# A mixture-of-experts and conditioning layer on one core: products on zeros ahead of the first input, later loads behind the decoded weights, routing and sorting in two groups of blocks

## The chip, the core and the metric

The kernel runs on one core of a Trainium2 chip. A core has five engines that run their own instruction streams beside each other: TensorE (matrix products, PE in the profile; PEld are its weight loads), VectorE (DVE), ScalarE (ACT), GpSimd (POOL) and SyncE (SP), which here only issues DMA transfers. The metric is the device time of one launch in microseconds; the median over several runs is given. A profile is one execution of its own, with a time of its own.

## The reference, cut to what matters

`x` has 128 sequences of 32 tokens with 128 features, 4096 tokens in all. Two layers are added to it.

```python
def _L0_cond_ref(x, mu, W_dec, b_dec, V):          # a weight matrix for each sequence
    U = (mu @ W_dec + b_dec).reshape(B, 129, 30)
    param = einsum('bik,kj->bij', U, V)
    return einsum('bsd,bde->bse', x, param[:, :-1, :]) + param[:, -1, :][:, None, :]

def _L0_ffn_ref(x, Wg, bg, W1, b1, W2, b2):        # 8 experts, the best 2 for each token
    topk_scores, topk_idx = top_k(xf @ Wg.T + bg, 2)
    w = softmax(topk_scores, axis=-1)
    h = gelu(einsum('td,ehd->teh', xf, W1) + b1)
    o = einsum('teh,eoh->teo', h, W2) + b2
    return einsum('tko,tk->to', take_along_axis(o, topk_idx[:, :, None], axis=1), w)

x = x + _L0_ffn_ref(_L0_cond_ref(x, cond_512, ...), ...)
x = x + _L1_ffn_ref(_L1_cond_ref(x, ids, ...), ...)
```

`_L1_cond_ref` is a chain of layernorms, table lookups by token ids and a two-layer network; `_L1_ffn_ref` is a gated network 128 to 512 to 512 to 512 to 128.

## The kernel before, in words

**Blocks.** The tokens are handled in 8 blocks of 512 (`TB`). For the first 3 blocks (`ND`) all 8 experts are computed densely ("dense experts", `experts`, L1143). For the other 5 (`NS`) the tokens are sorted by expert: each token's row of 64 values is scattered to `z_rows` in DRAM at the place of its expert, the experts run over their own rows (`sorted_expert`, L1189; it loads `zr`, makes `pzr`, `phs`, `py`, stores `y_rows`), and the results are gathered back (`combined`, L1252, `yg`). Then every block goes through `conditioning` (L1280) and `feed_forward` (L1418).

**The front.** It runs in these steps:

- Loads (L553 to L580): `mu_t` and `pre` on ScalarE's queue, all others on SP's, in this order: `w_dec` in two pieces, `x_t` in two pieces, `moe_w1`, `vecs`, `tabs`, `moe_w2`, `int_w1`, `st_in`, `wide_w2`, `b2_rows`, `tab_b`, a store of zeros to `z_rows`, and `tab_pw`. GpSimd clears the tile `zeros` (L575) first of all.
- Decoding (L617 to L639): four chunks of products `pu` of `w_dec` and `mu_t`, each with two PSUM tiles that VectorE and ScalarE copy to `u_sb`.
- `conditioned(i)` (L690) for each block: products `pz` of the block's `x_t` with `pre` and `u_sb` (outputs of 32 rows), VectorE's sum `zq`, products `pq` (which hold the block's 30 values a token and its 8 gate values), and for the first 3 blocks the transposes `p4_i` (shown as `p` in the profile) that give `z4`.
- `folded_all` (L665): four products `pwv` of `moe_w1`, 512 columns each, which ScalarE and VectorE turn into `w4`.
- Routing (L789) for blocks 0 to 2 and then once for blocks 3 to 7: VectorE adds the gate bias, finds the best two experts (`m_a`, `at_a`, `lo_a`, `hot_a`, then the same with `_b`), and `token_weights` (L826) makes their weights, with one `Exp` on ScalarE.
- `sorted_z` (L769) copies the values of blocks 3 to 7 out of `pq` to `z_tok`; `sorting` (L864) counts, for all 20 groups of 128 tokens at once, how many tokens go to each expert (`both`, two products `p_rank` and `p_count`, five doubling sums `sums`), and makes each token's row (`row_z` for the scatter, `row` for the gather).
- `scatters` (L954): 40 indirect DMAs on GpSimd, one for each 128 tokens and each of their two experts. A small memset `tick` behind each orders them.

**What sets the order.** All operations are recorded in a plan. `Plan.ordered` (L361) puts them in an order with a simple model of costs (`cost`, L307): at each step it takes, over all engines, the operation that can start first, and among those of one engine that can start within 20 ns the one with the lowest `prio`. The result is one fixed instruction stream for each engine. `prio` comes from where the code stands; in the front it is set by `in_order` (L90), which spreads the steps of a stream over a stretch, and after the front by the table `TIMES` (start and duration of each stream, L64), to which `T0` is added. Every operation shows line L472 in the profile, where the plan issues it, so the profile is read by the names of tiles.

**Pools.** `hid` and `work` open when the pool `setup` is done with, `exp` (the sorted experts' tiles) when `dense` (the dense experts' tiles) is done with (L545 to L547).

**Queues.** Each engine takes its instructions in order. SP's stream has all loads and stores of the table above, so that a transfer that has to wait holds those behind it. GpSimd's stream has the scatters, the gathers, the layernorms' short steps (`rs_st`, `rs_x`, `rs_h`, `rs_c`) and some halves of the feed-forward.

## Time and profile before

| | us |
|---|---|
| median of 6 runs | 440.23 |
| lowest and highest | 436.43, 443.36 |
| the profiled execution | 437.04 |
| its span, first to last instruction | 435.3 |
| mean granted TensorE clock | 0.965 |

Busy time in the span, with the number of instructions:

| engine | busy us | share | instructions |
|---|---|---|---|
| TensorE | 392.7 | 90% | 2102 |
| VectorE | 304.6 | 70% | 821 |
| ScalarE | 220.3 | 51% | 373 |
| GpSimd | 211.5 | 49% | 273 |

A row of the profile has a start and a duration in us, the engine, the operation, what it writes and reads (names without buffer numbers), and, in square brackets, how long the engine had been idle before and what released it. Rows of matrix products are pipelined and overlap, and their ends are modelled, so the sum of durations is more than the time. A float32 product shows as two instructions, a product of the type fp32r as one. The clock is shown as a share of full speed; before the first change of it in the trace, the column reads 1.00.

The whole span in 40 slices of 10.9 us, in tenths:

```
PE   6897698989899999999898899897899989999893
DVE  5566976896888845886779979997394685643501
ACT  4326255643464726454473446353466555466472
POOL 5025268888500100110488888786557245354351
PEclk 9558899999999999999999999999999999999998
DMA  8963531511104245452222313211000100000001
```

The scatters run from 52.0 to 112 us, the sorted experts' products from 146 to 208, the gathers from 212.5 to 302; the last block's store ends the span.

### The profile page before, as it was taken

To read this page: it belongs to the slowest core of one execution; us is meant where nothing else is said; L and a number is where in the kernel's file an instruction comes from. 1 tells how busy PE (TensorE), PEld (TensorE's weight loads), DVE (VectorE), ACT (ScalarE), POOL (GpSimd) and SP (SyncE) were. 2 spreads that over 40 slices of the span, in tenths; PEclk is the share of its full clock that TensorE was granted. 3 is DMA by queue.
4 is the path that set the end of the run, shared out by engine and by line. 5 is a ranking of instruction groups with operands and counts; after the bars stand their busy time and mean duration, and the time that the engine had idled before them with its cause. 6 is when DMAs were issued, how large, how long until landed. Compare 5 with 4: busy or idle time off the path is not lost.

```text
span 435.3 us, 6353 instructions
## 1 busy us (share of the span) xinstructions
PE 392.7 (90%) x2102; PEld 276.6 (64%) x2102; DVE 304.6 (70%) x821; ACT 220.3 (51%) x373; POOL 211.5 (49%) x273
## 2 busy tenths in 40 slices
PE   6897698989899999999898899897999989999893
PEld 5673354545467889878675477575677667576472
DVE  5566976896888845886779979997394685643501
ACT  4326255643464726454473446353466555466472
POOL 5025268888500100110488888786557245354351
PEclk9558899999999999999999999999999999999998
DMA  8963531511104245452222313211000100000001
GB/s 319 357 240 121 161 88 52 170 46 53 59 2 129 52 123 138 151 145 74 87 66 69 99 49 99 73 58 38 0 25 26 48 0 26 24 1 26 24 1 31
DMA packets 40249, 36.42 MB, mean 84 GB/s; under 512 B 20237, under 2 KB 31882, under 8 KB 39826
## 3 DMA queue, kind: packets, MB, share of 16 engines
q1 hardware_dynamic: 34642, 30.14, 21.7%
q0 software_dynamic: 2560, 3.94, 3.2%
q10 hardware_dynamic: 3008, 1.88, 1.4%
q8 instruction: 18, 0.29, 0.3%
q14 instruction: 21, 0.17, 0.1%
HBM read 21.13 MB, written 14.81 MB: 83 GB/s over the span
## 4 chain that ended last, share of the span: by engine, by line
PE 51%; DVE 19%; POOL 17%; issue 6%; DMA 3%; ACT 3%; DVEq 0%; SPq 0%; POOLq 0%; ACTq 0%
PE pgc L472 10%; POOL z_rows L472 8%; PE pgb L472 7%; PE pf L472 6%; PE pi L472 6%; PE py L472 6%; POOL yg L472 4%; PE po L472 3%; DVE h L472 3%; PE pz L472 2%; DMA yg<-y_rows,row 2%; DVE sl L472 2%; PE pu L472 2%; PE phs L472 2%; PE pzr L472 1%
## 5 line engine op out<-in xcount | busy, mean ns | idle before, releaser
L472 PE MATMUL po<-hw,moe_w_sb 128*128 128x512 f32 x96 | 48.3, 616 | 1.2 <-DVE hw L472 1.2
L472 POOL DMA_INDIRECT z_rows<-z_tok,row_z x40 | 40.4, 1010 | 17.7 <-DVE row_atz L472 9.5
L472 ACT ACTIVATE hs<-ph,vecs_sb 128x512 f32<-128x512 f32 x48 | 31.8, 685 | 27.8 <-PE ph L472 27.6
L472 POOL DMA_INDIRECT yg<-y_rows,row x40 | 41.1, 1028 | 9.5 <-issue 8.1
L472 PE MATMUL pgb<-ga_hi,f_h_hi 128*128 128x512 f32 x128 | 38.3, 410 | 4.1 <-DVE sl L472 3.7
L472 PE MATMUL pgc<-gb_hi,f_h_hi 128*128 128x512 f32 x128 | 38.5, 409 | 0.1
L472 POOL TENSOR_TENSOR ga_lo<-ga,ga_hi 128x512 fp32r<-128x512 f32 x18 | 23.0, 1278 | 31.4 <-ACT ga_hi L472 31.4
L472 PE MATMUL pgc<-gb_lo,f_h_hi 128*128 128x512 f32 x128 | 36.9, 400 | 0.3 <-DVE gb_lo L472 0.3
L472 DVE TENSOR_TENSOR hw<-hs,pbc 128x512 f32<-128x512 f32 x48 | 31.5, 679 | 7.5 <-PE pbc L472 7.0
L472 PE MATMUL pgb<-ga_lo,f_h_hi 128*128 128x512 f32 x128 | 36.2, 401 | 0.0
L472 ACT ACTIVATE gb<-pgb,vecs_sb 128x512 f32<-128x512 f32 x32 | 22.0, 688 | 25.9 <-PE pgb L472 25.9
L472 DVE SCALAR_TENSOR_TENSOR sl<-sl,pf 128x512 f32<-128x512 f32 x32 | 21.7, 679 | 18.8 <-ACT sl L472 18.8
L472 PE MATMUL pf<-cT_hi,f_w_hi 128*128 128x512 f32 x64 | 30.1, 470 | 5.0 <-DVE sl L472 2.0
L472 ACT CAST ga_hi<-ga 128x512 fp32r<-128x512 f32 x32 | 19.8, 617 | 25.8 <-DVE ga L472 25.8
L472 ACT ACTIVATE hss<-phs,vecs_sb 128x512 f32<-128x512 f32 (+1 forms) x32 | 19.4, 633 | 25.4 <-PE phs L472 25.2
L472 ACT ACTIVATE gc<-pgc,vecs_sb 128x512 f32<-128x512 f32 x32 | 21.7, 688 | 20.1 <-PE pgc L472 18.9
L472 PEld LDWEIGHTS pgb<-ga_hi,f_h_hi 128*128 128x128 f32 x128 | 22.9, 189 | 12.1 <-DVE sl L472 5.1
L472 PE MATMUL py<-moe_w_sb,hss 128*128 128x128 f32 x224 | 30.0, 276 | 0.0
L472 PEld LDWEIGHTS py<-moe_w_sb,hss 128*128 128x128 f32 x224 | 28.1, 191 | 2.9 <-issue 1.6
L472 ACT ACTIVATE sl<-pf,half_w1s 128x512 f32<-128x512 f32 x32 | 22.0, 687 | 13.4 <-PE pf L472 12.3
L472 POOL TENSOR_TENSOR gc_lo<-gc,gc_hi 128x512 fp32r<-128x512 f32 x18 | 22.9, 1289 | 11.9 <-ACT gc_hi L472 11.3
L472 POOL TENSOR_TENSOR rs_c<-mv_c,eps 128x4 f32<-128x4 f32 x8 | 1.8, 227 | 53.9 <-DVE mv_c L472 53.8
(271 smaller groups left out, 964.5 us busy)
## 6 DMA issues: line engine op xcount, KB each, us to landing
moe_w_sb<-in_moe_w_dram SPq DMA_DIRECT2D x2, 1024.0 KB
f_h_raw<-in_f_h_dram SPq DMA_DIRECT2D x8, 256.0 KB
kept_x<-x1T SPq DMA_DIRECT2D x8, 256.0 KB
kept_c<-cT SPq DMA_DIRECT2D x8, 256.0 KB
zr<-z_rows SPq DMA_DIRECT2D x16, 128.0 KB
y_rows<-y SPq DMA_DIRECT2D x8, 256.0 KB
out_dram<-o SPq DMA_DIRECT2D x8, 256.0 KB
pid<-in_pid_dram SPq DMA_DIRECT2D x8, 250.0 KB
```

The costliest lines, as they stand in the source:

```text
L472: result = getattr(getattr(self.tc.nc, op.engine), op.method)(*args, **kw)
```

## The change

- **Products on zeros.** A tile `idle_in` is cleared by VectorE, and 12 products of 128x512 (type fp32r) on it are recorded: 8 ahead of everything and one at the end of each of the four decoding chunks. Their output `idle_out` is used by nobody. In the program that the plan makes of it, 11 of them stand ahead of the first `pu` and one behind the first 8 products `pu`.
- **Later loads behind decoding.** The tile `zeros` is now cleared by VectorE, behind its last copy to `u_sb` (`cut`). The store of zeros is in two, the first expert's rows and the other seven's, and all loads from `moe_w1` on are ordered behind the first of them (`gate`). In SP's order the loads `xT`, `pid` and `id` of blocks 0 and 1 now stand ahead of that store, and `moe_w1` and the others behind it.
- **Two groups.** `sorted_z`, `routing` and `sorting` run for blocks 3 and 4 and then for blocks 5 to 7. `sorting` takes the counts of the earlier group (`so_far`) and adds them to its first column. Both counting products go to one PSUM tile. Three or four doubling sums replace five. The first 16 scatters need the first group's rows alone.
- **Order.** All 8 `conditioned(i)` are spread at steps of 0.5, with `folded_all` from 0.6 to 4.6, routing of blocks 0 to 2 comes behind in `prio`; 18 entries of `TIMES` change; the model's factor of 2 for TensorE in the front and its DMA rate change; the PSUM tile of `pwT` moves to another tag.

```diff
+GROUPS = ((ND, 5), (5, NB))
...
-    "experts0": (-0.4, 0.9),
-    "second_layer": (0.29, 0.8),
+    "experts0": (-1.07, 0.9),
+    "second_layer": (-0.06, 0.8),
-    "scatters": (0.47, 0.66),
+    "scatters": (0.64, 0.66),
-    "experts2": (1.59, 0.79),
-    "experts1": (0.21, 1.24),
+    "experts2": (1.59, 0.8),
+    "experts1": (0.09, 1.24),
-    "sorted": (0.27, 0.29),
-    "cond1": (2.7, 0.55),
+    "sorted": (0.27, 0.28),
+    "cond1": (2.7, 0.33),
-    "cond3": (3.44, 1.29),
-    "cond5": (5.8, 1.2),
-    "cond6": (6.87, 1.11),
+    "cond3": (3.44, 1.42),
+    "cond5": (5.91, 0.75),
+    "cond6": (6.61, 0.79),
-    "ffn4": (5.39, 1.04),
-    "ffn5": (7.66, 0.38),
+    "ffn4": (6.5, 0.88),
+    "ffn5": (7.66, 0.2),
...
-            elif op.prio[0] < T0:
-                busy *= 2
...
-            return (450.0 if op.engine == "sync" else 500.0), 2200.0 + size / 180.0
+            return (450.0 if op.engine == "sync" else 500.0), 2200.0 + size / 350.0
...
+    gate, cut = [], [None]
+
     def load(name, shape, src=None, eng=None, pool=const):
         t = pool.tile(list(shape), F32, tag=name, name=f"{name}_sb")
-        (eng or nc.sync).dma_start(t, a[name] if src is None else src)
+        op = (eng or nc.sync).dma_start(t, a[name] if src is None else src)
+        if gate:
+            plan.behind(op, gate[0])
         return t
...
-    w1_t = load("moe_w1", [D, E * H], pool=setup)
...
-    z_rows = kept.tile([E * ALL, 2 * KZ], F32, tag="z_rows", name="z_rows")
-    zeros = setup.tile([P, CAP // P * 2 * KZ], F32, tag="zeros", name="zeros")
-    nc.gpsimd.memset(zeros, 0.0)
-    nc.sync.dma_start(
-        z_rows.rearrange("(e r) k -> e r k", e=E)[:, :CAP].rearrange("e (p c) k -> p e (c k)", p=P),
-        zeros.unsqueeze(1).to_broadcast([P, E, CAP // P * 2 * KZ]),
-    )
-    pw_f = load("tab_pw", [VPW, 2 * D], pool=setup)
...
+    idle_in = setup.tile([P, TB], F32R, tag="idle", name="idle")
+    nc.vector.memset(idle_in.bitcast(F32), 0.0)
+    idle_out = ps_acc("idle")
+    def idle(n):
+        for _ in range(n):
+            nc.tensor.matmul(idle_out, idle_in[:, :P], idle_in, start=True, stop=True)
+    idle(8)
...
+        idle(1)
         for h in range(2):
             dst = u_sb[:, :, h * KH + k0 : h * KH + k0 + n].rearrange("p b k -> p k b")
             src = pu[h][:, : n * B].rearrange("p (k b) -> p k b", k=n)
             if h:
                 nc.scalar.copy(dst, src)
             else:
-                nc.vector.tensor_copy(dst, src)
+                cut[0] = nc.vector.tensor_copy(dst, src)
...
+    z_rows = kept.tile([E * ALL, 2 * KZ], F32, tag="z_rows", name="z_rows")
+    zeros = setup.tile([P, CAP // P * 2 * KZ], F32, tag="zeros", name="zeros")
+    plan.behind(nc.vector.memset(zeros, 0.0), cut[0])
+    z_first = z_rows.rearrange("(e r) k -> e r k", e=E)[:, :CAP]
+
+    def no_rows(e0, e1):
+        return nc.sync.dma_start(
+            z_first[e0:e1].rearrange("e (p c) k -> p e (c k)", p=P),
+            zeros.unsqueeze(1).to_broadcast([P, e1 - e0, CAP // P * 2 * KZ]),
+        )
+
+    gate.append(no_rows(0, 1))
+    w1_t = load("moe_w1", [D, E * H], pool=setup)
+    vecs = load("vecs", [P, NVEC])
+    tabs = load("tabs", [4 * E, NTAB], pool=setup)
+    w2_t = load("moe_w2", [P, E, NH * D], a["moe_w2"].rearrange("e p n -> p e n"))
+    plan.behind(no_rows(1, E), gate[0])
+    int_w1 = load("int_w1", [P, 6, D], a["int_w1"].rearrange("(i p) j -> p i j", p=P))
+    st_in = load("st_in", [P, 5, D], pool=dense)
+    wide_w2 = load("wide_w2", [D, 4, D], pool=dense)
+    b2_rows = load("b2_rows", [P, 3 * D], a["b2_rows"].partition_broadcast(P), pool=dense)
+    tab_b = load("tab_b", [D, 3, P], pool=dense)
+    pw_f = load("tab_pw", [VPW, 2 * D], pool=setup)
...
-    def sorted_z():
+    def sorted_z(i0, i1):
+        t = z_tok[:, i0 - ND : i1 - ND]
         for q in range(4):
-            z = pq[q][:, : NB * (KZ + E)].rearrange("p (i n) -> p i n", i=NB)[:, ND:, :KZ]
-            nc.scalar.copy(z_tok[:, :, q, 0, :], z)
-            nc.vector.tensor_tensor(
-                z_tok[:, :, q, 1, :], z, z_tok[:, :, q, 0, :], ALU.subtract
-            )
+            z = pq[q][:, : NB * (KZ + E)].rearrange("p (i n) -> p i n", i=NB)[:, i0:i1, :KZ]
+            nc.scalar.copy(t[:, :, q, 0, :], z)
+            nc.vector.tensor_tensor(t[:, :, q, 1, :], z, t[:, :, q, 0, :], ALU.subtract)
         nc.scalar.dma_start(
-            z_kept.rearrange("(c p) k -> p c k", p=P),
-            z_tok.rearrange("p i c r k -> p (i c) (r k)").bitcast(F32),
+            z_kept.rearrange("(c p) k -> p c k", p=P)[:, (i0 - ND) * NC : (i1 - ND) * NC],
+            t.rearrange("p i c r k -> p (i c) (r k)").bitcast(F32),
...
-    def sorting(hots):
-        n, h = NS * NC, hots
-        both = setup.tile([P, n, E], F32R, tag="both", name="both")
+    def sorting(i0, i1, hots, so_far):
+        n, h = (i1 - i0) * NC, hots
+        here = slice((i0 - ND) * NC, (i1 - ND) * NC)
+        both = setup.tile([P, n, E], F32R, tag=f"both{i0}", name=f"both_{i0}")
         nc.vector.tensor_tensor(both, h[0], h[1], ALU.add)
         flat = both.rearrange("p c e -> p (c e)")
-        pr = ps_mm("p_rank")
-        nc.tensor.matmul(pr[:, : n * E], before, flat, start=True, stop=True)
-        pn = ps_ff("p_count")
-        nc.tensor.matmul(pn[:, : n * E], ones_r, flat, start=True, stop=True)
-        src, dst = sums
-        nc.vector.tensor_copy(src[:, PRE:], pn[:, : n * E].rearrange("p (c e) -> p c e", e=E))
+        p = ps_mm(f"p_rank_{i0}")
+        pr, pn = (p[:, k : k + n * E].rearrange("p (c e) -> p c e", e=E) for k in (0, TB // 2))
+        for dst, w in ((pn, ones_r), (pr, before)):
+            nc.tensor.matmul(dst.rearrange("p c e -> p (c e)"), w, flat, start=True, stop=True)
+        src, dst = sums[i0]
+        nc.vector.tensor_copy(src[:, PRE:], pn)
+        if so_far is not None:
+            nc.vector.tensor_tensor(src[:, PRE], src[:, PRE], so_far, ALU.add)
         d = 1
         while d < n:
             nc.vector.tensor_tensor(
...
             )
             src, dst = dst, src
             d *= 2
-        row = setup.tile([P, n, E], F32, tag="row", name="row")
-        nc.vector.tensor_tensor(
-            row,
-            pr[:, : n * E].rearrange("p (c e) -> p c e", e=E),
-            src[:, PRE - 1 : PRE - 1 + n],
-            ALU.add,
-        )
-        row_z = setup.tile([P, n, E], F32, tag="row_z", name="row_z")
+        row = setup.tile([P, n, E], F32, tag=f"row{i0}", name=f"row_{i0}")
+        if so_far is not None:
+            nc.vector.tensor_copy(src[:, PRE - 1], so_far)
+        nc.vector.tensor_tensor(row, pr, src[:, PRE - 1 : PRE - 1 + n], ALU.add)
+        row_z = setup.tile([P, n, E], F32, tag=f"row_z{i0}", name=f"row_z_{i0}")
         nc.vector.scalar_tensor_tensor(
             row_z, iota_e.to_broadcast([P, n, E]), float(ALL), row, ALU.mult, ALU.add
         )
...
             row, row, float(CAP - 1), first_row.to_broadcast([P, n, E]), ALU.min, ALU.add
         )
         for name, src_row, dsts in (("z", row_z, row_best_z), ("y", row, row_best)):
+            plan.prio += 0.1
             for j in range(2):
-                at = setup.tile([P, n, E], F32, tag="row_at", name=f"row_at{name}{j}")
+                at = setup.tile([P, n, E], F32, tag="row_at", name=f"row_at{name}{j}_{i0}", bufs=2)
                 nc.vector.tensor_tensor(at, src_row, h[j], ALU.mult)
-                row_f = setup.tile([P, n], F32, tag=f"row_f{j}", name=f"row_f{name}{j}")
+                row_f = setup.tile([P, n], F32, tag=f"row_f{j}", name=f"row_f{name}{j}_{i0}")
                 nc.vector.tensor_reduce(row_f, at, AX.X, ALU.add)
-                nc.vector.tensor_copy(dsts[j], row_f)
-        nc.vector.tensor_reduce(most, src[:1, PRE + n - 1], AX.X, ALU.max)
+                nc.vector.tensor_copy(dsts[j][:, here], row_f)
+        return src[:, PRE + n - 1]
...
+    sums = {}
+    for i0, i1 in GROUPS:
+        sums[i0] = [
+            setup.tile([P, PRE + (i1 - i0) * NC, E], F32, tag=f"sums{i0}{j}", name=f"sums{j}_{i0}")
+            for j in range(2)
+        ]
+        for t in sums[i0]:
+            nc.gpsimd.memset(t, 0.0)
...
     folding = folded_all()
+    plan.prio = 0.0
     next(folding)
-    in_order(plan, *((float(i), 1.5, 2, conditioned(i)) for i in range(ND)))
-    routed = routing(0, ND)
-    token_weights(*routed[:4], routed[4:])
     in_order(
         plan,
-        *((float(i), 1.5, 2, conditioned(i)) for i in range(ND, NB)),
-        (2.0, 6.0, 4, folding),
+        *((float(i), 0.5, 2, conditioned(i)) for i in range(NB)),
+        (0.6, 4.0, 4, folding),
     )
     for _ in folding:
         pass
-    routed = routing(ND, NB)
-    sorted_z()
-    sorting(routed[4:])
-    token_weights(*routed[:4], None)
+    plan.prio = ND + 0.1
+    routed = routing(0, ND)
+    token_weights(*routed[:4], routed[4:])
+    count = None
+    for i0, i1 in GROUPS:
+        plan.prio = i1 - 1.0
+        routed = routing(i0, i1)
+        count = sorting(i0, i1, routed[4:], count)
+        plan.prio -= 0.05
+        sorted_z(i0, i1)
+        plan.prio += 0.1
+        token_weights(*routed[:4], None)
+    nc.vector.tensor_reduce(most, count[:1], AX.X, ALU.max)
...
-        pw = ps_tp(f"pwT_{i}")
+        pw = ps_mm(f"pwT_{i}")
```

More of the change, by code (lines that the diff above doesn't have):

```diff
@@ L62 @@
 TIMES = {
-    "experts0": (-0.4, 0.9),
-    "second_layer": (0.29, 0.8),
+    "experts0": (-1.07, 0.9),
+    "second_layer": (-0.06, 0.8),
     "weights": (-1.45, 0.1),
-    "scatters": (0.47, 0.66),
+    "scatters": (0.64, 0.66),
     "count": (1.57, 0.05),
-    "experts2": (1.59, 0.79),
-    "experts1": (0.21, 1.24),
+    "experts2": (1.59, 0.8),
+    "experts1": (0.09, 1.24),
     "cond0": (0.01, 0.57),
-    "sorted": (0.27, 0.29),
-    "cond1": (2.7, 0.55),
+    "sorted": (0.27, 0.28),
+    "cond1": (2.7, 0.33),
     "ffn0": (2.63, 0.71),
     "ffn1": (3.7, 0.48),
-    "cond2": (3.07, 0.5),
-    "cond3": (3.44, 1.29),
-    "cond4": (4.9, 0.15),
-    "cond5": (5.8, 1.2),
-    "cond6": (6.87, 1.11),
-    "cond7": (8.68, 2.47),
-    "ffn2": (4.08, 1.18),
-    "ffn3": (5.29, 0.12),
-    "ffn4": (5.39, 1.04),
-    "ffn5": (7.66, 0.38),
-    "ffn6": (8.62, 0.86),
-    "ffn7": (9.35, 0.52),
+    "cond2": (3.19, 0.5),
+    "cond3": (3.44, 1.42),
+    "cond4": (4.9, 0.17),
+    "cond5": (5.91, 0.75),
+    "cond6": (6.61, 0.79),
+    "cond7": (8.68, 2.47),
+    "ffn2": (4.08, 1.2),
+    "ffn3": (5.42, 0.12),
+    "ffn4": (6.5, 0.88),
+    "ffn5": (7.66, 0.2),
+    "ffn6": (8.62, 0.73),
+    "ffn7": (9.52, 0.52),
 }
@@ L562, in adaln_ffn_kernel @@
         x_t += [x_some[:, i * TB : (i + 1) * TB] for i in range(i1 - i0)]
-    w1_t = load("moe_w1", [D, E * H], pool=setup)
-    vecs = load("vecs", [P, NVEC])
-    tabs = load("tabs", [4 * E, NTAB], pool=setup)
-    w2_t = load("moe_w2", [P, E, NH * D], a["moe_w2"].rearrange("e p n -> p e n"))
-    int_w1 = load("int_w1", [P, 6, D], a["int_w1"].rearrange("(i p) j -> p i j", p=P))
-    st_in = load("st_in", [P, 5, D], pool=dense)
-    wide_w2 = load("wide_w2", [D, 4, D], pool=dense)
-    b2_rows = load("b2_rows", [P, 3 * D], a["b2_rows"].partition_broadcast(P), pool=dense)
-    tab_b = load("tab_b", [D, 3, P], pool=dense)
-    z_rows = kept.tile([E * ALL, 2 * KZ], F32, tag="z_rows", name="z_rows")
-    zeros = setup.tile([P, CAP // P * 2 * KZ], F32, tag="zeros", name="zeros")
-    nc.gpsimd.memset(zeros, 0.0)
-    nc.sync.dma_start(
-        z_rows.rearrange("(e r) k -> e r k", e=E)[:, :CAP].rearrange("e (p c) k -> p e (c k)", p=P),
-        zeros.unsqueeze(1).to_broadcast([P, E, CAP // P * 2 * KZ]),
-    )
-    pw_f = load("tab_pw", [VPW, 2 * D], pool=setup)
+    idle_in = setup.tile([P, TB], F32R, tag="idle", name="idle")
[5 more added lines that the diff above has]
+    idle(8)
     iota_p = iota([P, 1], [[0, 1]], 1, "iota_p")
@@ L826, in token_weights @@
     def token_weights(n, here, m1, m2, hots):
-        e2 = setup.tile([P, n], F32, tag=f"e2{n}", name=f"e2_{n}")
+        e2 = setup.tile([P, n], F32, tag=f"e2{here.start}", name=f"e2_{here.start}")
         nc.vector.tensor_tensor(e2, m2, m1, ALU.subtract)
@@ L914, in adaln_ffn_kernel @@
     PRE = 16
-    sums = [
-        setup.tile([P, PRE + NS * NC, E], F32, tag=f"sums{j}", name=f"sums{j}") for j in range(2)
-    ]
-    for t in sums:
-        nc.gpsimd.memset(t, 0.0)
+    sums = {}
[6 more added lines that the diff above has]
+            nc.gpsimd.memset(t, 0.0)
     most = const.tile([1, 1], F32, tag="most", name="most")
```

## The prediction

> **What bounds the kernel now.** I read the page's chain first, then the span in 10 us windows, then the front at finer grain, then single rows. The chain by engine:
>
> ```profile
> PE 51%; DVE 19%; POOL 17%; issue 6%; DMA 3%; ACT 3%; DVEq 0%; SPq 0%; POOLq 0%; ACTq 0%
> ```
>
> TensorE carries half of it, but that is an average over stages. The busy table (us and count for each engine, granted clock, DMA) of the first 60 us, the part that the change touches:
>
> ```profile
> 0.00:10.00 10.00, 6.09 (x58) 5.63 (x59) 5.86 (x12) 3.85 (x4) 6.27 (x28) 1.00 0.82 311
> 10.00:20.00 10.00, 8.66 (x164) 6.58 (x162) 4.56 (x20) 2.83 (x11) 0.00 (x0) 0.62 1.06 356
> 20.00:30.00 10.00, 10.00 (x172) 7.09 (x172) 7.79 (x52) 2.36 (x9) 1.36 (x3) 0.50 0.83 302
> 30.00:40.00 10.00, 8.47 (x90) 4.80 (x90) 4.75 (x15) 6.26 (x13) 5.64 (x6) 0.69 0.46 153
> 40.00:50.00 10.00, 6.40 (x14) 3.32 (x15) 9.81 (x35) 4.68 (x7) 2.42 (x2) 0.83 0.52 156
> 50.00:60.00 10.00, 8.05 (x32) 4.79 (x31) 8.95 (x40) 4.32 (x9) 4.76 (x9) 1.00 0.10 34
> ```
>
> Three stages show. Up to 12 us decoding (pu, u_sb). From 12.2 to 36.6 the chain lies on TensorE alone, at half clock: pz 8.9 us of it, pq 5.5, pwv 4.0, the transposes p 3.5, ph 1.2. From 36.6 to 55.0 it lies on VectorE (routing, sorting), while TensorE idles some 7 us. From there to 210 TensorE is idle only 7 us in all, then 11 us in 200 to 300, where VectorE is over 9 of 10 busy, and 10 us in the tail.
>
> The clock: granted 0.67 in 12:13, 0.88 in 36:37, 0.74 in 46:47, 0.56 in 49:50, so it fell at 12.34, rose at 36.24, fell at 46.48, rose at 49.88. The gaps are 23.90, 10.24 and 3.40 us, seven, three and one times 3.41: a fixed window decides. These are such windows (columns as above):
>
> ```profile
> 8.92:12.34 3.42, 3.03 (x37) 2.53 (x36) 1.80 (x5) 1.76 (x3) 0.00 (x0) 1.00 1.00 423
> 39.65:43.06 3.41, 1.85 (x6) 1.05 (x6) 3.32 (x11) 2.47 (x5) 2.77 (x2) 1.00 0.15 55
> 43.06:46.48 3.42, 1.11 (x5) 0.48 (x3) 3.36 (x12) 1.89 (x3) 0.00 (x0) 1.00 0.40 86
> 29.41:32.83 3.42, 3.42 (x64) 2.50 (x64) 0.99 (x2) 0.99 (x2) 2.37 (x4) 0.50 0.27 102
> 32.83:36.24 3.41, 3.41 (x16) 1.21 (x18) 0.99 (x2) 1.52 (x2) 1.85 (x2) 0.50 0.07 6
> ```
>
> The first was 3.03 us busy and the clock fell after it; the second only 1.85, and it stayed. The fourth was busy throughout without a rise; the fifth, filled by 512-column pwv and ph, raised it. So narrow products (32 or 40 columns, 64 rows) count little, wide ones much, and a rise asks for more than staying up does.
>
> **The change part by part.** Sums are made against the profiled execution: span 435.3, 437.04 with what lies around it; the median shown, 440.23, is 3.2 above that.
>
> *Idle products.* Eleven of the twelve 128x512 products stand ahead of all decoding in the changed program's order, one after the first chunk. They can start after VectorE's memset of their operand (GpSimd's 128x512 memset took 0.52; VectorE's first instruction now is at 1.42, waiting for iota_p), so at about 1.3 us. Price of one, nearest rows: 0.24 at full clock (32 pgb in 7.74 us), 0.60 at half (two ph in 1.21). Eleven last 2.7 to 6.6 us and end between 4.0 and 7.9; decoding began at 3.88, when mu_t landed. The delay is 0.1 to 4.0 us, plus 0.2 to 0.6 for the twelfth. Given back: the 0.33 us wait for the second w_dec, and what a raised clock takes off the 7.9 us of decoding; u_sb copies of 1.04 us each stand between its chunks, so I allow at most 2.3. Bounds -2.0 to +4.6; I take +0.5, the clock rising midway.
>
> *What the clock then gives.* If the raised clock lasts through 12.2 to 36.6, prices come from pairs of rows on both sides of the rise:
>
> ```profile
> 31.64 0.67 PE L472 MATMUL pq<-zg,zq 32*128 32x40 f32 x8
> 36.07 0.49 PE L472 MATMUL pq<-zg,zq 32*128 32x40 f32 x8
> 28.04 2.08 PE L472 MATMUL pwv<-moe_w_sb,pre_sb 128*128 128x512 f32 x2
> 36.48 1.13 PE L472 MATMUL pwv<-moe_w_sb,pre_sb 128*128 128x512 f32 x2
> ```
>
> pq: 7 x 0.18 = 1.3. pwv: 2 x 0.95 = 1.9. Four transposes took 1.05 to 1.25 at half, 0.63 (pwT) at full: 3.54 - 1.89 = 1.6. ph 1.21 - 0.50 = 0.7. pz has no row at full clock: between nothing and half of 8.9, 4.4. Sum 5.5 to 9.9. VectorE was busy 13.4 us in this stage and gets some 2.5 more, 16 in a stage of 17 to 19, so it begins to hold: I take 6.0, near the low end. If the clock falls as it did at 12.34: 0.
>
> Before the fall at 12.34 no gap on TensorE was longer than 0.39 us: the row says that a window full of narrow products can lower the clock, so I leave open whether it is kept. The Trainium skill speaks against that row: TensorE: Matmul & The Clock Gate (Part 1, "What's actually happening") has the clock raised by one busy window of about 3.4 us and lowered by an idle one. By that rule a raised clock would stay up here and the whole of this term would come.
>
> *Loads behind decoding.* The zeros memset waits for VectorE's last u_sb copy (ended 12.78), and SP's queue holds at the zero fill behind it; moe_w1, vecs, tabs, moe_w2 and the rest stand behind. Ahead of it SP now passes two xT, two pid, two id. moe_w1 (1 MB behind 0.2 MB) would land at about 13.5 + 3.1 (what mu_t took) + 1.2 MB at 380 GB/s = 19.8. Its reader pwv stands after block 4's pq, at 25.8 now and some 22 with a full clock: covered by 2 to 6 us; without that cover up to 2 us. The large zero fill lands after moe_w2, near 31, and the first scatter comes past 42: covered. Earlier w_dec: nothing, TensorE waited 0.33 us for it.
>
> *Routing and sorting in two groups.* Between block 7's zq and the first hw_2, VectorE ran 71 instructions in 19.7 us (35.3 to 55.0). The changed order has 87 there, narrower. Prices:
>
> ```profile
> 46.90 0.32 DVE L472 TENSOR_TENSOR sums<-sums 128x160 f32<-128x160 f32 x1
> 22.49 0.26 DVE L472 TENSOR_TENSOR at_a<-g,m_a 128x96 f32<-128x96 f32 x1
> ```
>
> A 160-wide one of 0.32 follows the last by 0.235 when others lie between; with the same 0.085 overlap 96-wide ones cost 0.17, 64-wide 0.13. 32 x 0.17 + 21 x 0.13 + four hw at 0.60 + one w 0.69 + three at 0.25 + 26 small at 0.11 = 14.9: 4.8 less. With no overlap (0.26, 0.22, 0.15) it is 20.9: 1.2 more. I take -3.0: the two groups interleave, as hw and int_w did before. ScalarE loads two more tables (1.28 each); its 6.9 us idle before st_act near 47 hides them; if that is gone, 2.6.
>
> *Scatters.* Group one's rows come some 7 us after block 7's zq, so the first scatter moves from 52.0 to about 43 and the last (111) to about 98. This buys little, for the reader waits for something else:
>
> ```profile
> L472 SPq DMA_DIRECT2D zr<-z_rows x32: 517/524/654, 130.9 to 199.6; - x32
> ```
>
> Its first load came 19 us after the last scatter, when the dense experts (last hs 130.8) gave up their pool. What is left is that the layernorm steps rs_x, rs_h, rs_c no longer queue on GpSimd between scatters: 0 to 3 us of TensorE's 5 us idle in 60 to 120; I take 1.
>
> *Start times.* The streams after 60 us get new order; TensorE's idle time after 200, 25 us, bounds it. No row prices it: -4 to +4, I take 0.
>
> Sum with the clock held: +0.5 - 6.0 - 3.0 - 1.0 = -9.5. Span 425.8, median 430.7.
>
> **The rivals.**
> A (forecast): the clock rises early and is kept. For: 1.85 us of wide work kept it at 39.65; the pwv lie closer together now. Against: narrow work lost it at 12.34. 427.5 profiled, 430.7 median; with its terms at their nearer bounds 425 to 436.
> B: the clock falls when decoding ends, as before. Decoding +1.5, clock 0, sorting -3, scatters -1: -2.5, median 437.7 (434 to 441).
> C, slower: the idle products stay at half clock, 0.60 each, and hold the decoding behind them on TensorE: +4.6 at 4 us; sorting without overlap +1.2; no gain elsewhere: +5.8, median 446. It decides when the rise comes later than the eleventh product's end and sorting's narrow steps do not overlap.
> D: the new order after 60 us gives back what the front gained: between 436 and 445, median 440.
>
> **How the numbers follow.** A measurement here tells 1% (4.4 us: 435.8 and 444.6) from no change. A 0.52, of it 0.48 faster, 0.03 same, 0.01 slower. B 0.30: 0.13, 0.15, 0.02. C 0.11: 0, 0.01, 0.10. D 0.07: 0.02, 0.04, 0.01. Together faster 0.63, same 0.23, slower 0.14. The range 423 to 443 takes in A with pz at its far bound, B and most of D, and leaves out C and the ends of A; A's own is 425 to 436.
>
> **What would show it.** Right: clock 1.00 through most of 12 to 30 and pq of 8 near 0.49; first hw_2 near 46; first scatter by 43, the last near 98, zr still waiting for the dense experts. Wrong: 0.50 again from some window near 12 until pwv (then B); pu starting past 6 us (towards C); pwv waiting on moe_w1; TensorE's idle time in 200 to 300 above 15 us (D).

## The result and the profile after

The changed kernel takes 453.86 us (447.05 to 457.0, 20 runs) against 440.24 (435.73 to 443.75, 46 runs): 1.024 times the time of before, 95% interval 1.021 to 1.028 (the ratio leaves disturbed runs out, the medians don't). Slower by 2.4%, where 430.7 was forecast. The page's span and its chain of waits, by engine:

```profile
span 444.7 us, 6423 instructions
...
PE 59%; DVE 26%; issue 5%; POOL 4%; ACT 3%; DMA 2%; ACTq 0%; DVEq 0%; POOLq 0%
```

GpSimd has almost left the chain (4%, 17% before): the scatters, which carried it from 63 to 112 us, no longer do. TensorE and VectorE have taken its place. The front in 10 us windows (columns as in the prediction):

```profile
10.00:20.00 10.00, 8.67 (x204) 6.50 (x204) 5.88 (x27) 2.98 (x15) 0.00 (x0) 0.91 0.86 267
20.00:30.00 10.00, 8.86 (x146) 5.04 (x145) 8.15 (x41) 3.56 (x9) 5.25 (x6) 0.75 1.07 358
30.00:40.00 10.00, 6.32 (x76) 3.77 (x75) 8.21 (x43) 8.33 (x16) 4.47 (x3) 0.93 0.49 162
40.00:50.00 10.00, 7.53 (x19) 3.96 (x19) 9.41 (x52) 4.71 (x9) 5.83 (x11) 0.56 0.91 266
```

The clock did rise early (at 4.50 us) and 10 to 20 us has 0.91 where it had 0.62. But VectorE is now over 8 of 10 busy from 20 us on, and TensorE idles 4.8 us in 20 to 40 (1.5 before): the last zq ends at 34.2 instead of 35.3.

In spite of that small gain the sorted experts' last product, py, ends at 198.3 instead of 208.6, 10.3 us earlier. The loss lies behind it. Two windows there, first of the kernel before, then of the changed one:

```profile
200.00:250.00 50.00, 44.61 (x210) 31.57 (x209) 41.38 (x112) 25.13 (x41) 32.23 (x34) 1.00 0.26 81
250.00:300.00 50.00, 44.14 (x205) 31.96 (x204) 46.26 (x130) 24.94 (x42) 42.89 (x44) 1.00 0.22 66
```

```profile
200.00:250.00 50.00, 44.93 (x170) 30.86 (x170) 43.62 (x121) 22.68 (x37) 37.28 (x39) 0.86 0.24 74
250.00:300.00 50.00, 43.35 (x193) 31.87 (x191) 44.06 (x117) 25.26 (x41) 39.23 (x40) 0.97 0.19 56
```

TensorE is as busy as before while its clock fell (0.86, 0.97). The counts, 363 products instead of 415, are not of the same work: 45 of the 415 are the sorted experts' products up to 208.6 us (py, pzr, phs, 41 of them with 128 columns), which the changed kernel had finished, and of products with 512 columns both kernels make as many (257 and 255). Counted in the first 100 us behind each kernel's own last py the loss shows: 357 products instead of 385, of those with 512 columns 253 instead of 278, in 87.2 us of busy time instead of 88.7. Busy time alone hides it. From the end of the last py to the end of TensorE's last product the kernel before needs 221.3 us, the changed one 240.5. I add up from the trace, for that stretch, when TensorE had a product running, when none, and when its clock was at half:

| kernel | stretch | busy | idle | of it at half clock | products |
|---|---|---|---|---|---|
| before | 221.3 | 201.9 | 19.4 | 0 | 861 |
| changed | 240.5 | 213.3 | 27.2 | 17.1 | 888 |

So +19.2 = 11.4 of busy time + 7.8 of waits. The busy time I split by pricing each product at what those of its name and shape add to busy time on average in the kernel before. The 27 products more (one block's pi, 18; four ph, one pg_h, four pf), which the kernel before does ahead of its last py, come to 7.0. The 35 that begin at half clock took 16.5 instead of 9.7: 6.9. All others took 2.5 less. So some 7 of the 10.3 us by which the last py is earlier are work that has only moved behind it. Four of the changed kernel's waits, from its timeline; the bracket is the idle time in front of the product and what ended it:

```profile
200.45 0.51 PE L472 MATMUL pf<-cT_hi,f_w_hi 128*128 128x512 f32 x1 [1.93 <-DVE sl L472]
...
234.56 1.11 PE L472 MATMUL ph<-ident,h 128*128 128x128 f32 x4 [3.41 <-DVE sc_t L472]
...
270.38 0.48 PE L472 MATMUL pg_t<-oh,tab_g 128*128 128x512 f32 x1 [2.11 <-DVE h L472]
...
302.93 0.87 PE L472 MATMUL pc<-ident,ch 128*128 128x128 f32 x3 [3.35 <-DVE ch L472]
```

Behind 60 us the kernel before has no wait over 1.41 us. The second of these (3.41) comes in good part from GpSimd's queue: rs_h, without which h can't be normalised, has its first step at 229.19, then a gather of 1.44, and only then its second, which took 1.69 where most take 1.0, beside a subtraction of VectorE (gc_lo, at 231.16):

```profile
229.19 0.27 POOL L472 TENSOR_TENSOR rs_h<-mv_h,eps 128x4 f32<-128x4 f32 x1 [1.30 <-DVE mv_h L472]
...
229.60 1.44 POOL L472 DMA_INDIRECT yg<-y_rows,row  x1
...
231.06 1.69 POOL L472 TENSOR_TENSOR rs_h<-rs_h,mhalf 128x4 f32<-128x4 f32 x1
...
232.79 1.26 DVE L472 TENSOR_SCALAR h<-h,mv_h,rs_h 128x128 f32<-128x128 f32 x4 [0.94 <-POOL rs_h L472]
```

And what such waits do to the clock. These are 3.41 us windows of the changed kernel; the clock fell after the first four and stayed after the last:

```profile
14.74:18.15 3.41, 2.95 (x69) 2.09 (x62) 1.68 (x11) 0.98 (x6) 0.00 (x0) 1.00 0.95 309
199.07:202.48 3.41, 1.98 (x8) 1.09 (x8) 3.33 (x10) 1.19 (x2) 1.21 (x2) 1.00 0.38 131
229.78:233.19 3.41, 1.37 (x6) 0.61 (x4) 2.47 (x9) 1.67 (x3) 3.19 (x3) 1.00 0.24 58
267.33:270.74 3.41, 1.30 (x7) 0.75 (x6) 3.38 (x9) 0.28 (x1) 3.26 (x3) 1.00 0.00 0
298.05:301.46 3.41, 1.53 (x7) 0.91 (x5) 3.41 (x10) 1.71 (x3) 3.41 (x4) 1.00 0.01 2
```

So a wait of 2 to 3.4 us costs itself, and behind three of these four came one or two windows at half clock (6.83, 6.83 and 3.41 us); the fourth, from 299.58 to 302.93, lies across the end of a window, and the clock stayed. The Trainium skill (TensorE: Matmul & The Clock Gate, "What's actually happening") says that the window runs freely, so that the same kernel meets it at another phase each time; that would agree with what is seen here, though no run moves the phase alone: over the changed kernel's 22 recorded executions the span goes from 445.3 us at a mean clock of 0.965 to 455.2 at 0.928. With the clock at either 1 or half, this mean gives each execution's time at half clock: 37 us in the profiled one, 56 in the median. The span grows by 0.31 us for each such us (a straight line through all 22; 0.24 through the eight shortest). The profiled execution (446.61) lies 7.25 below the median, and by that slope some 6 of it are clock. The profile thus shows less of the loss than the median has.

### The profile page after: what moved, and what is told of

It reads as the page before. It is cut to its first block, busy times and chain, and to the rows that moved or that the text cites. A ratio compares the mean times of both kernels' runs of the same rounds, so it can differ in the third digit from the quotient of the medians.

```text
span 444.7 us, 6423 instructions
## 1 busy us (share of the span) xinstructions
PE 398.1 (90%) x2116; PEld 278.2 (63%) x2116; DVE 315.9 (71%) x867; ACT 225.3 (51%) x380; POOL 213.7 (48%) x274
## 4 chain that ended last, share of the span: by engine, by line
PE 59%; DVE 26%; issue 5%; POOL 4%; ACT 3%; DMA 2%; ACTq 0%; DVEq 0%; POOLq 0%
PE pgc L472 10%; PE pgb L472 9%; PE pf L472 8%; PE pi L472 7%; PE po L472 6%; PE py L472 6%; DVE h L472 4%; DVE sl L472 2%; DVE x L472 2%; PE ph L472 2%; DVE ga L472 2%; POOL z_rows L472 2%; PE pzr L472 1%; PE phs L472 1%; DMA yg<-y_rows,row 1%
## 5 line engine op out<-in xcount | busy, mean ns | idle before, releaser
L472 PE MATMUL po<-hw,moe_w_sb 128*128 128x512 f32 x96 | 49.5, 618 | 2.0 <-DVE hw L472 2.0
L472 POOL DMA_INDIRECT yg<-y_rows,row x40 | 42.1, 1054 | 12.1 <-issue 8.3
L472 ACT ACTIVATE hs<-ph,vecs_sb 128x512 f32<-128x512 f32 x48 | 32.1, 686 | 30.3 <-PE ph L472 26.5
L472 PE MATMUL pf<-cT_hi,f_w_hi 128*128 128x512 f32 x64 | 31.7, 495 | 9.5 <-DVE sl L472 6.5
L472 ACT ACTIVATE sl<-pf,half_w1s 128x512 f32<-128x512 f32 x32 | 22.0, 688 | 23.2 <-PE pf L472 19.7
L472 ACT CAST ga_hi<-ga 128x512 fp32r<-128x512 f32 x32 | 19.7, 617 | 20.0 <-DVE ga L472 19.8
L472 PEld LDWEIGHTS pgc<-gb_lo,f_h_hi 128*128 128x128 f32 x128 | 24.1, 191 | 8.2 <-DVE gb_lo L472 1.7
L472 PEld LDWEIGHTS pgb<-ga_lo,f_h_hi 128*128 128x128 f32 x128 | 24.0, 188 | 6.1 <-DVE ga_lo L472 0.8
```

Source lines behind the costliest of these rows:

```text
L472: result = getattr(getattr(self.tc.nc, op.engine), op.method)(*args, **kw)
```

## The experiments

Theories, stated ahead of the runs: O, the order that the planner gave the conditioning and feed-forward steps made the stretch long; F, sorted experts that lie closer together leave work and gaps behind, whatever the order; H, the products on zeros and the clock raised early make it fall later; D, block 2's conditioning standing behind all py products leaves TensorE too little to do there. To move one thing at a time, the conditioning and feed-forward steps of all blocks were "held" in a given kernel's order on each engine:

```
for k in order_of_the_given_kernel:
    op = late_ops[k]
    plan.behind(op, last_on[op.engine])
    last_on[op.engine] = op
```

Summary, times in us; the columns on the stretch behind the last py are from the profiled execution, made as above (e2's is its longest, 4.3 above its median). The last column counts the products in that stretch, the useless ones of e5 and e12 included: where it differs, the last py isn't a like mark. Each median stands beside a kernel before of 437.8 to 440.1.

| run | median | last py ends | stretch | busy | idle | half clock | products |
|---|---|---|---|---|---|---|---|
| e1_late_before | 452.67 | 205.5 | 237.5 | 213.8 | 23.7 | 3.4 | 902 |
| e2_late_after | 464.32 | 210.0 | 251.3 | 221.4 | 30.0 | 34.1 | 908 |
| e3_no_idle | 453.74 | 200.2 | 244.0 | 215.5 | 28.5 | 23.9 | 888 |
| e4_one_group | 457.28 | 197.7 | 251.1 | 224.6 | 26.5 | 28.0 | 925 |
| e5_hold | 449.83 | 201.0 | 243.6 | 219.8 | 23.8 | 14.7 | 921 |
| e6_swap_after | 444.42 | 200.8 | 233.6 | 211.6 | 22.0 | 13.7 | 888 |
| e7_swap_before | 431.44 | 206.9 | 218.6 | 202.3 | 16.3 | 0 | 861 |
| e8_old_plan | 455.74 | 217.4 | 228.9 | 207.5 | 21.4 | 6.8 | 859 |
| e9_cond2 | 448.63 | 201.8 | 239.8 | 216.8 | 23.1 | 20.5 | 890 |
| e10_late_pe | 452.80 | 197.7 | 248.0 | 218.9 | 29.1 | 27.3 | 899 |
| e11_idle_before | 439.22 | 207.6 | 226.7 | 206.4 | 20.3 | 7.7 | 861 |
| e12_swap_hold | 440.15 | 197.8 | 230.9 | 213.8 | 17.1 | 0.6 | 911 |
| e15_new_plan | 450.30 | 199.9 | 242.6 | 216.1 | 26.4 | 23.9 | 888 |
| e16_cond2_swap | 441.33 | 201.3 | 234.0 | 215.1 | 18.9 | 17.8 | 890 |

**The orders exchanged.** First the changed kernel held to the order of before, then the kernel before held to the changed order, then the changed kernel with TensorE alone held.

> The changed kernel, with the conditioning and feed-forward steps of all blocks held, on each engine, in the order in which the kernel before has them; everything else as in the changed kernel. Theory O (the loss lies in the order that the planner gave those steps): the last py still ends near 198 to 202, the stretch from there to TensorE's end goes back from 240.5 to 221 to 226, no fall of the clock after 60 us, span 420 to 428, median 425 to 434. Theory F (sorted experts that lie closer together leave work and gaps behind, whatever the order): the stretch stays over 234, median 445 to 457. Theory H (the products on zeros and the clock raised early make it fall later): the clock still falls two or three times between 195 and 280, median 438 to 450.

> The kernel before, with the conditioning and feed-forward steps in the changed kernel's order; decoding, routing, sorting, scatters and loads as before. Theory O: the front as before (last py 205 to 212), the clock falls after 190 us, the stretch behind the last py is 232 to 243, median 448 to 462. Theory F or H: the stretch stays at 221 to 226 without a fall, median 437 to 445.

> The changed kernel with TensorE alone held to the kernel before's order of conditioning and feed-forward products; the other engines are ordered by the planner. The first gather then needn't wait as it did when all engines were held (224.5 there, 18 us behind the last y_rows). Theory D or O: the stretch behind the last py is 222 to 230 and the median 430 to 442, if the last py stays near 200; theory F: over 234, median 446 to 460.

None of the three gave a short time: 1.033 (1.026 to 1.041), 1.055 (1.047 to 1.064) and 1.031 (1.025 to 1.038) times before. The changed order makes the stretch long on the old front too (251.3, for O), but the old order doesn't make it short on the new one (237.5 and 248.0, against O as first stated). In e1 GpSimd held the first gather behind the old order's earlier layernorms: it came at 224.5, 18 us after the last y_rows. Moved by itself, neither order fitted the other front, and these runs don't separate O from F.

**The parts of the code.** The first diff takes the products on zeros out of the changed kernel, the second sorts in one group; both with the changed order held. The third puts the products alone into the kernel before, with its order held.

```diff
-    idle(8)
...
-        idle(1)
```

```diff
-GROUPS = ((ND, 5), (5, NB))
+GROUPS = ((ND, NB),)
```

```diff
+    idle(8)
     iota_p = iota([P, 1], [[0, 1]], 1, "iota_p")
...
+        idle(1)
         for h in range(2):
```

> The changed kernel without its twelve products on zeros and their memset; the order of the conditioning and feed-forward steps is held as in the changed kernel. If the forecast's clock term is right, the clock is 0.50 from about 12 until a pwv comes, and the last py comes 4 to 8 us later than 198.3 (decoding, which no longer waits for the eleven products, may give 1 back). Theory O and F: the stretch behind the last py stays at 235 to 243, median 452 to 462. Theory H: the clock doesn't fall between 195 and 280, the stretch is 222 to 230, median 436 to 446.

> The changed kernel with blocks 3 to 7 routed and sorted as one group (one item in GROUPS), the order of the conditioning and feed-forward steps held as in the changed kernel. If the forecast's terms for sorting and scatters are right, first scatter 50 to 54 instead of 44, last scatter 107 to 112, last py 3 to 5 later than 198.3, and the stretch behind it unchanged: median 2 to 5 above the changed kernel's 453.9. If the two groups cost as much as they save, the last py within 1.5 us of 198.3 and the median within 2 us.

> The kernel before with the twelve products on zeros alone (eight ahead of decoding and four behind its first chunk in this order), its order of conditioning and feed-forward steps held. By the forecast's clock term the stage from 12 to 36 us gets 5.5 to 9.9 shorter at a held clock, decoding 0 to 4 longer: median 431 to 439. If VectorE, not TensorE, sets the pace of that stage once the clock is up, or the clock falls again by 20 us, the front gains under 2.5 us and the median is 437 to 444.

Without the products the last zq is 2.3 us later (36.46) and the last py 1.9 later, but the median is the same (453.74). In the kernel before they gain 1.2 at the last zq and 1.0 at the last py; the ratio is 1.0006 (0.9965 to 1.0047; one of e11's ten executions took 2072.66 us, which nothing here explains). H falls: the clock falls behind 200 us without them as well. One group moves the scatters back (first 53.9, last 111.2; with two 43.1 and 99.6) and the last py doesn't follow: 197.7, even 0.6 earlier, but with 37 more products left behind it. Its median is 3.4 above the changed kernel's, in the range that the terms for sorting and scatters gave, but not by the way that they gave (a later last py), and its four executions (450.65 to 459.83) lie across those of the changed kernel. So what the two groups are worth stays open.

e11 also shows the fall of the clock by itself. It has the order and the 861 products of before in that stretch, and its five longest waits there are the same within 0.02 us; but the clock fell at 232.1 and 354.9 and 0.8 us before the end, where in the profile of before it didn't. 7.7 us at half clock came with 4.5 us more busy time. The 22 products that began at half clock took 7.9 us instead of 4.4, so 3.5 of the 4.5 are theirs (prices as above).

**Waits filled.** Products of no use ahead of the four waits, with the order held:

```diff
+bank = ps_bc(f"hold{k}")
+for _ in range(holds[k]):
+    h = nc.tensor.matmul(bank, ones_r, ff_w["f_h1"][:, 0], start=True, stop=True)
+    plan.behind(h, last_on["tensor"])
```

> The changed kernel with its order held, and 33 products on finished weights (128x512, result unused) put into TensorE's stream at the four places where it waited longest between the last py and 303 us: 5 ahead of the feed-forward product at 200.45, 11 ahead of the ph at 234.56, 6 ahead of the pg_t at 270.38, 11 ahead of the pc at 302.93. They fill waits of 1.9 to 3.4 us. If the falls of the clock come from these waits and cost half of the 17.1 us spent at half clock, the clock doesn't fall between 195 and 305 us, the stretch behind the last py drops from 240.5 to 231 to 235 and the median to 443 to 449. If the falls are only a sign of something else, the median stays at 451 to 457 or rises by what the products take.

The clock stayed up from 51 to 283 us, then fell at 283, 362 and 420, at other waits. The median is 449.83: 4.0 less, between the two ranges. The stretch didn't drop (243.6 in the profiled execution, the longest of the four, where 231 to 235 were expected), and the ratio to before, 1.021 (1.014 to 1.029), can't be told from the changed kernel's 1.024 (1.021 to 1.028). So this run shows that the waits at the four places go with the falls there, and that there are more places than four; what a fall costs it doesn't show. For that there are the products at half clock above and the spread of one kernel's executions.

**VectorE beside GpSimd.** Some VectorE operations of the changed kernel took several times as long as their like. From the timeline:

```profile
264.50 1.30 POOL L472 TENSOR_TENSOR gc_lo<-gc,gc_hi 128x512 fp32r<-128x512 f32 x1
264.73 2.48 DVE L472 SCALAR_TENSOR_TENSOR x<-yg,w_best,x 128x128 f32<-128x128 f32 x1
...
265.75 1.29 POOL L472 TENSOR_TENSOR cT_lo<-cT,cT_hi 128x512 fp32r<-128x512 f32 x1
```

The x (0.34 as a rule) started beside one subtraction of GpSimd and ended as a second one was over. Summed behind 195 us, what VectorE's operations took over their median (those over by more than 0.15) is 19.7 us in the changed kernel, in 19 operations, and 13.4 before, in 18; a subtraction of GpSimd lies beside each. The edit moves those subtractions (20 in the changed kernel, 18 in the kernel before) to VectorE:

```diff
         lo = hid.tile([P, TB], F32R, tag=f"{tag}lo", name=f"{name}_lo", bufs=bufs)
+        if name in ON_VECTOR:
+            eng = nc.vector
```

> The changed kernel with its order held, and the 20 subtractions of halves (128x512, 1.3 us each on GpSimd) beside which a VectorE operation of this kernel's profile took 0.4 to 2.1 us longer than its like, moved to VectorE (0.69 each there). If those VectorE operations waited for GpSimd's subtraction (19.7 us in all behind 195 us, against 13.4 in the kernel before), VectorE is busy some 6 us less there, hardly any of its normalising steps takes over 0.5 us, TensorE's waits of over 1.5 us behind 260 us shrink, and the median falls to 443 to 450. If the long durations are waits for something else, they stay, VectorE gets 14 us more to do, and the median rises to 455 to 465.

> The same edit in the kernel before, with its own order held: the 18 subtractions beside which a VectorE operation took longer than its like, moved to VectorE. If VectorE waits for GpSimd's subtraction, its 13.4 us of such waits go and 12.4 us of work come: the median falls by 0 to 4 us, to 434 to 440. If not, it rises by 3 to 12.

The same place in e6, where gc_lo and cT_lo now run on VectorE:

```profile
263.65 0.68 DVE L474 TENSOR_TENSOR gc_lo<-gc,gc_hi 128x512 fp32r<-128x512 f32 x1
...
264.25 0.35 DVE L474 SCALAR_TENSOR_TENSOR x<-yg,w_best,x 128x128 f32<-128x128 f32 x1
...
265.06 0.66 DVE L474 TENSOR_TENSOR cT_lo<-cT,cT_hi 128x512 fp32r<-128x512 f32 x1
```

Nearly all of the overlong time is gone: 1.2 us of 19.7 are left, and 0.4 of 13.4 in the kernel before. The changed kernel gains 9.4 us (444.42), the kernel before 8.7 (431.44; 0.981 times its time, 0.973 to 0.989). That is the fastest version of the study. But both gain alike: these waits are a loss of both kernels and not the difference between them. A rival for the gain is that GpSimd has some 20 us less to do behind the last py, and its queue gets shorter; no run separates the two. Against it speaks that VectorE's idle time behind the last py that ended with GpSimd fell only from 6.0 to 4.3 us in the kernel before and from 4.8 to 3.5 in the changed one.

**Both together**, on the changed kernel:

> The changed kernel with its order held, the same 20 subtractions moved to VectorE, and 23 products on finished weights ahead of the four places where TensorE still waited over 1.4 us then: 6 ahead of the feed-forward product at 202.98 in that run, 8 ahead of the ph at 236.44, 4 ahead of the pc at 296.94, 5 ahead of the feed-forward product at 407.87. If half of the 13.7 us at half clock behind the last py was the price of those waits, the clock doesn't fall at 204 and 409, the stretch goes from 233.6 to 226 to 230 and the median from 444.4 to 437 to 442. If it falls elsewhere instead, the median stays at 442 to 447. In neither case below 434: the 27 products that are left over behind the last py (2.9 us) and the remaining short waits stay.

440.15, 1.003 (0.999 to 1.007) times before. Its windows:

```profile
200.00:250.00 50.00, 45.62 (x188) 30.64 (x189) 45.48 (x129) 24.38 (x40) 37.28 (x38) 1.00 0.25 76
250.00:300.00 50.00, 46.81 (x215) 34.56 (x215) 42.64 (x133) 27.06 (x45) 31.00 (x32) 1.00 0.17 56
```

403 products (12 of the useless ones among them) where the changed kernel made 363, with the last py at the same place within 0.6 us; no fall from 49 us to 428. The median is 4.3 below e6's, the intervals of the two ratios (e6: 1.004 to 1.018) just overlap. With the waits filled and the clock kept, the changed kernel is back at the time of before, but not below it, nor near before's own 431.44 with the same edit of GpSimd.

**Numbers or code.** The change also alters 18 entries of the start times and two estimates in the cost function. e8 is the changed code with the old numbers, e15 the old code with the new numbers; the planner orders both.

> The changed kernel's code (products on zeros, loads behind decoding, two groups) with the start times and the cost estimates of the kernel before: nothing held, the planner orders it. If the new start times and costs are what made the stretch behind the last py long, it is 221 to 228 and the median 428 to 438. If any front other than the one for which the start times were chosen makes that stretch long, it stays over 232 and the median is 442 to 460.

> The kernel before's code with the changed kernel's start times and cost estimates, once more. In the disturbed run the stretch behind the last py was 247.7, and the waits of 1.9 to 3.5 us at the same pf, ph, pg_t, pxh and pc as in the changed kernel were there. If the numbers make the stretch: last py 200 to 207, stretch 236 to 246, median 448 to 458 beside a kernel before of 438 to 441. If the code does: stretch 220 to 228, median under 445.

The new numbers on the old code give the result: 1.024 (1.015 to 1.034) times before, the last py at 199.9, the stretch 242.6 with the same 888 products in it, and the waits at the same pf, ph and pc as above (and at pxh, 1.60 in the changed kernel), from its timeline:

```profile
202.10 0.53 PE L470 MATMUL pf<-cT_hi,f_w_hi 128*128 128x512 f32 x1 [1.94 <-DVE sl L470]
...
236.07 0.68 PE L470 MATMUL ph<-ident,h 128*128 128x128 f32 x4 [3.37 <-DVE sc_t L470]
...
279.71 0.33 PE L470 MATMUL pxh<-ident,xh 128*128 128x128 f32 x1 [2.02 <-DVE xh L470]
...
303.10 0.87 PE L470 MATMUL pc<-ident,ch 128*128 128x128 f32 x3 [3.38 <-DVE ch L470]
```

The new code with the old numbers has a short stretch (228.9, just over the expected 221 to 228) and a late py (217.4), and is slow by another way, which wasn't traced: its median of 455.74, 1.040 (1.030 to 1.049) times before, misses the expected 428 to 438. So O holds in this form: the new numbers, without any of the code, make both the early py and the long stretch; the code adds nothing that can be measured on top of them. Which of the 18 start times and two estimates does it wasn't separated. e15 also does in the front what the products on zeros were for: without any, its clock stayed up from 7.87 to 28.35 us, and its last zq ended at 33.9 (34.2 in the changed kernel). A first run of this kernel and of the next one (e13_new_plan, e14_cond2_swap) took 467.63 and 460.99 us (1.042, 1.020 to 1.064, and 1.020, 0.979 to 1.061, times before) beside a kernel before of 445 to 461 us, with waits of up to 7.9 us at 60 to 80 us that the profile puts down to nothing on the core; they are left out, and e15 and e16 repeat them.

**Block 2's place.** In the kernel before, block 2's pi stands behind 84 of the 112 py products on TensorE, in the changed kernel behind all. One start time moves it to 64:

```diff
-    "cond2": (3.19, 0.5),
+    "cond2": (2.7, 0.5),
```

> The changed kernel with one start time altered: the conditioning of block 2 starts at 2.7 (over 0.5) instead of 3.19, and the planner orders everything anew; its pi then stands after 64 of the 112 py products instead of behind all of them, its last transposes (pc) after 106, and feed-forward products of blocks 0 and 1 are left for later in exchange. Theory D (behind the last py TensorE has little but block 1's feed-forward, because block 2's conditioning stands behind all of the sorted experts; it then waits for that conditioning's chain, and the clock falls): no wait of TensorE over 1.5 us and no fall of the clock between 195 and 245 us, the stretch behind the last py 226 to 236, median 438 to 449. If what TensorE has to do there makes no difference, the median stays at 450 to 458.

> The changed kernel with block 2's conditioning started earlier and 17 colliding subtractions on VectorE, once more. If the order around the last py and VectorE's waits are separate losses, the median is 438 to 442; if they are one and the same, 443 to 448.

448.63 by itself, 5.2 less (1.019 times before, 1.010 to 1.027), and 441.33 with its own 17 colliding subtractions moved, 3.1 below e6 (1.004 times before, 0.999 to 1.008, against e6's 1.011, 1.004 to 1.018): less each time, as D has it, but with intervals that overlap. e9's profile still has a fall at 211.7, which D excluded, 20.5 us at half clock in all, a stretch of 239.8 where D said 226 to 236, and its median is at the end of D's range. D may be a part of the loss; it isn't its whole.

## Why the prediction was wrong

- **Products on zeros**: right. They ended at 5.64; the first pu began at 5.57 instead of 3.88, and the last u_sb copy ended at 12.61 instead of 12.77: -0.2 where +0.5 was taken. The clock rose midway, as assumed.
- **What the clock gives**: the mechanism was right, the size was not. -6.0 was taken from pairs of TensorE's rows; the last zq came 1.1 us earlier, and the products alone are worth 1.2 to 2.3 there. The prediction said that VectorE "begins to hold" and chose "near the low end" of 5.5 to 9.9. Three things took the rest: in 12 to 36 us 2.8 us of TensorE's idle time ended with a result of VectorE, 6.8 us were at half clock, and all eight pwv now begin ahead of the last zq's end, where in the kernel before four did. The clock was neither kept (A) nor lost at 12 us (B): it fell at 18.15, after a window with 2.95 us of mostly narrow products, and rose at 24.98. The Trainium skill's rule that an idle window lowers it (TensorE: Matmul & The Clock Gate, "What's actually happening") doesn't fit that fall. The prediction's reading that narrow products count little doesn't come out either: the window before, 11.33 to 14.74, was less busy (2.54 us), with products as narrow (82 of 107 have 32 or 40 columns, against 47 of 59), and the clock stayed up.
- **Loads behind decoding**: right at nothing. The first pwv started at 22.0, as estimated, and later ones waited for VectorE's w, not for the load.
- **Sorting, scatters**: right in place (first scatter 43.1 against 43, last 99.6 against 98; the third expert's hw at 52.4 instead of 55.0, where 46 was named) and right that the scatters' earlier end buys little: zr still waited for the dense experts. Sorting's -3.0 isn't seen: first hw and last py got little or nothing of it, and the run with one group leaves its worth open. In the sum without overlap, which rival C uses, the terms add up to 20.7 and not 20.9.
- **Start times**: the step that failed. "The streams after 60 us get new order; TensorE's idle time after 200, 25 us, bounds it. No row prices it: -4 to +4, I take 0." Idle time bounds what a better order can gain; it doesn't bound what a worse one can lose. The new numbers alone (start times and the two estimates) moved the last py by -8.6 and the stretch behind it by +21.3, in e15's profile against that of before: +12.7 where at most 4 was allowed, and +12.5 in the medians (450.30 against 437.81). The first of these lay outside the range as well, so that the forecast of -9.5 looks met at 198.3 us (-10.3) by luck. The other terms, -9.5 together, brought nothing that can be measured on top of it: 1.024 times before with the code and without. And the reading beside this term was off: in 200 to 300 us VectorE was not over 9 of 10 busy but 87.6 of 100 us.
- **Rival D** named the mechanism ("gives back what the front gained") but let it give back only that: 436 to 445 at 0.07. Its sign, over 15 us of idle time in 200 to 300, didn't show either: it was 11.7, in part because products at half clock count as busy. The count of like products behind the last py, or the clock column, would have shown it.

What stays open: why the loss of the new order is as large as it is. Of the 19.2 us in the profiled execution 7.8 are waits, some 7 are products moved behind the last py, and some 7 are half clock, less 2.5 elsewhere. The medians differ by 13.6, the profiled executions by 9.6. In the sessions on chips 1, 4 and 6 the kernel before is at half clock for 32 to 40 us in the median, the changed kernel for 56; at 0.31 for each us that is an estimate of 5 to 7 of the 13.6. The waits were traced for ph (a gather ahead of rs_h's second step), for pg_t (VectorE held by GpSimd), and only in part for the others. No order was found that has the early py and the short stretch together.

## What to carry to other kernels

Where the whole instruction order comes from a table of start times, an edit of that table is the largest part of the change, even if it looks like retuning: it asks for a range of its own on both sides, and a run with the table alone. A wait of 2 us on TensorE should be priced with the clock that it may lower, not at its length alone; count products of one width per window beside busy time. Look for VectorE operations that take several times their like, and for what GpSimd does beside them, before moving anything else: here moving what GpSimd did there was worth 2% in either kernel.

## What the runs showed of the hardware

VectorE operations waited for whole GpSimd operations: a 128x128 one of 0.34 us took 0.6 to 1.5 beside a subtraction of 1.3 us (half of them 1.2 to 1.4), 1.86 and 2.02 where a shorter GpSimd operation stood ahead of the subtraction, and 2.48 where a second subtraction followed. The Trainium skill (SBUF — State Buffer, "Who interferes with whom") says that a VectorE instruction with two inputs in SBUF contends with a GpSimd instruction that reads SBUF, and one in a 2-port mode with GpSimd, and that the second to come is blocked for a whole instruction; e6 and e7 agree, with 19.7 us reduced to 1.2 and 13.4 to 0.4.

The clock's fall follows no single threshold of busy time: it fell after 1.98 us of 3.41 and stayed after 1.53, and fell after 2.95 of mostly narrow products though it had stayed after 2.54 of products as narrow. In one order of instructions (the kernel before and e11, behind the last py) it fell in one execution and not in another, with the five longest waits equal within 0.02 us.
